# A gate for every gather in a graph network's edge loop

## The chip, the cores and the metric

The kernel runs on one core of a Trainium2 chip. The metric is the time of one execution on the device, in microseconds (us), as the median of several runs.

## The reference

One layer of a graph network on 6250 nodes with 256 features and 206250 edges, sorted by their destination. All numbers are 32-bit floats.

```
h    = relu(layernorm(x))
e    = relu(raw @ W_e1.T + b_e1) @ W_e2.T + b_e2          # raw: 64 features of an edge
edge = (e * (clip(polarity, 0, 1) + 0.01)) @ W_le.T + b_le
msg  = relu(h[src] + edge)                                # one row gathered for each edge
aggr = segment_sum(msg, dst)
g    = layernorm((h + aggr) @ W_g1.T + b_g1) * ln_g + ln_b
out  = x + relu(g) @ W_g2.T + b_g2
```

## The kernel before

**Staging.** A first stage normalizes the nodes and writes `relu(layernorm(x)) + b_le` to a table in HBM, `hb_d`. W_e2 and W_le are multiplied into one matrix `wc_s`. The edges are cut into 403 blocks of 512 edges (4 tiles of 128). A *unit* is half a block, 256 edges; there are NU = 806 units, and the edge loop goes once through them. Two blocks make a pair (4 units), 6 blocks make a group, whose sums come out together. `LEAD` = 22 units are computed ahead, during the first stage.

**The work of a unit.** `edge_part(u)` runs 8 matmul instructions on TensorE (L268) into a PSUM tile `pz`, which VectorE empties into `msg` (L273). Every pair needs a first layer on TensorE before (`first_layer`, L245), which fills four `pz` tiles; ScalarE (L253) and VectorE (L250) empty them. In the middle of the loop (`by_two`) first layers come for two pairs at once, every 8 units: this is called a *turn* here, and its run of L245 has 16 instructions and needs 8 tiles. There are 7 `pz` tiles. Behind the first layers of a turn stand the sums of two pairs (`add_pairs`, `add_up`, L583: 8 instructions a block) and the loads of two more pairs (`load_pair`, on SyncE's queue).

**The gathers.** Each unit needs two indirect DMAs of 128 rows from `hb_d` into a tile `hg` (L531), issued by GpSimd. `whole(u)` then adds the gathered rows to the messages on VectorE (L566, twice a unit, in place in `hg`) and applies relu on ScalarE (L571); the sums on TensorE (L583) read `hg`, and then its buffer is free. There are `HG` = 16 buffers of two gathers.

**The order of work.** The order on each engine is the order in which the program is written; no scheduler moves anything. An engine carries out its instructions in order, and waits where a semaphore has not come far enough. In the loop over u, `forward(u)` writes the unit's matmuls (and the turn's, when it is one), then `gathers(...)` writes the gathers that are now due, then `whole(made)` follows for a unit that lies behind u by a distance that shrinks from 22 to 1 in the course of the loop, and `due()` writes at most one step of the nodes' work (TensorE's L682, L166, L182, L192), which starts when the sums of a group are there.

**The gates.** `gathers(last, behind)` issues gathers up to unit `last`. The first gather of a call gets a made-up dependency on `behind`, here `last_z`, the last matmul of the unit: GpSimd may not start it sooner. In the middle of the loop the limit is

```
k = (u - TURN) % 8
gathers(4 * summed + HG - 8 + (1, 2, 3, 4, 5, 6, 6, 7)[k], last_z)
```

so that gathers are issued for buffers that the sums have freed, spread over the 8 units of a turn. Before the loop, `gathers(HG)` issues the first 32 gathers without a gate. In the last 24 units gathers have no gate either. Beside the gate a gather waits for its buffer, and for the landing of the gather 8 places before it.

Of the kernel before, what the change touches and what calls it, by code (L numbers as in the profile page):

```python
# [17 lines left out]
P = 128  # L18
N = 6250
D = 256  # L20
F = 64
# [7 lines left out]
S = 4  # L29
L = 6  # L30
W = 32
# [7 lines left out]
DEG = E // N  # L39
LEAD = 22  # L40
LEAST = 1
SHRINK = 36
HG = 16
FEW = 6
QUIET = (0, 1)
TURN = 1
# [5 lines left out]
def group_of(b):  # L52
    return b // L


def blocks_of(g):
    return range(g * L, min((g + 1) * L, NB))
# [36 lines left out]
def gnn_kernel(ctx: ExitStack, tc: tile.TileContext, x, src_c, dst_c, dst_r, pol_c, raw_t, w_e1t, w_e2,  # L94
               w_let, w_g1t, w_g2t, vec_c, row_v, x_t, out):
    nc = tc.nc
# [3 lines left out]
    hb_d = dram.tile([N, D], F32, name="hb_d")  # L100
# [14 lines left out]
    we1_s = const.tile([P, D], F32, name="we1_s")  # L115
    wc_s = const.tile([P, 2, D], F32, name="wc_s")
    bc_s = const.tile([P, 2, D], F32, name="bc_s")
    src_s = const.tile([P, NT], I32, name="src_s")
# [92 lines left out]
    NU = 2 * NB  # L211
    fast = ExitStack()
    fast.enter_context(tc.manual_schedule())
    with fast:
# [8 lines left out]
        raw, sel, e1, hg, msg, ms = {}, {}, {}, {}, {}, {}  # L223
        pd = psd.tile([P, 2, D], F32, name="pd")

        def ps():
            return psz.tile([P, 2, D], F32, name="pz")
# [6 lines left out]
        def first_layer(q):  # L234

            bs = [b for b in (2 * q, 2 * q + 1) if b < NB]
            if not bs:
                return
            for b in bs:
                e1[b] = e1_p.tile([P, 2, 512], F32, name="e1")  # L240
            pe = {}
            for c in range(2):
                for s, b in enumerate(bs):
                    pe[s, c] = ps().rearrange("p a b -> p (a b)")
                    nc.tensor.matmul(pe[s, c], we1_s[s * F:(s + 1) * F, c * P:(c + 1) * P],  # L245
                                     raw[q][s * F:(s + 1) * F, :], start=True, stop=True)
            for c in range(2):
                for s, b in enumerate(bs):
                    if s == c == 1:
                        nc.vector.tensor_scalar(e1[b][:, c, :], pe[s, c], be1_s[:, c:c + 1], 0.0, op0=ALU.add,  # L250
                                                op1=ALU.max)
                    else:
                        nc.scalar.activation(e1[b][:, c, :], pe[s, c], AF.Relu, bias=be1_s[:, c:c + 1])  # L253
            raw.pop(q)

        def plain(u):

            return u < LEAD and u % 3 == 1

        def edge_part(u):  # L260

            nonlocal last_z
            b, v = divmod(u, 2)
            pz = ps()
            for i in range(2):
                k = (2 * v + i) * P
                for c in range(2):
                    last_z = nc.tensor.matmul(pz[:, i, :], e1[b][:, c, k:k + P], wc_s[:, c, :], start=c == 0, stop=c == 1)  # L268
            msg[u] = msg_p.tile([P, 2, D], F32, name="msg")
            if plain(u):  # L270
                nc.scalar.activation(msg[u], pz, AF.Copy)
            else:
                nc.vector.tensor_add(msg[u], pz, bc_s)  # L273
            if v == 1:
                e1.pop(b)

        last_z = None
        sums = lambda last: None

        def by_two(q):  # L280
            return FEW <= q < NP - FEW
# [16 lines left out]
        def forward(u):  # L298

            edge_part(u)  # L300
            if u % 4 == TURN:
                turn_of(u // 4)
# [33 lines left out]
        with tc.tile_pool(name="p1", bufs=4) as p1, tc.tile_pool(name="p1x", bufs=11) as p1x:  # L336
# [76 lines left out]
            for k in range(len(parts) + 1):  # L413
# [15 lines left out]
                for _ in range((k > 0) + (k > 2 and k % 3 > 0)):  # L429
                    u = next(units, None)  # L430
# [85 lines left out]
        with tc.tile_pool(name="hg", bufs=HG) as hg_p, tc.tile_pool(name="ms", bufs=5) as ms_p, \  # L516
                tc.tile_pool(name="sel2", bufs=9) as sel2_p, tc.tile_pool(name="nd", bufs=3) as nd:
            got = 0
            acc = {}
            made = 0  # L520
            summed = 0

            def gathers(last, behind=None):

                nonlocal got
                while got < min(NU, last):
                    u = got
                    got += 1
                    hg[u] = hg_p.tile([P, 2, D], F32, name="hg")
                    for i in range(2):  # L530
                        g = nc.gpsimd.indirect_dma_start(  # L531
                            out=hg[u][:, i, :], out_offset=None, in_=hb_d,
                            in_offset=bass.IndirectOffsetOnAxis(ap=src_s[:, 2 * u + i:2 * u + i + 1], axis=0))
                        if behind is not None:
                            tc.add_manual_dep(g.ins, behind.ins.name, mybir.DependencyInfo(
                                mybir.DependencyClass.Sync, mybir.DependencyReason.DATA), reason="gathers in step with PE")
                            behind = None

            def select(g):

                return [(g, lambda k=k: rows_of_block(g, k)) for k in range(len(blocks_of(g)))]

            def rows_of_block(g, k):

                t = (g * L + k) * S
                if k == 0:
                    sel[g] = sel_p.tile([P, L * S, W], F32, name="sel")
                nc.vector.scalar_tensor_tensor(  # L548
                    sel[g][:, k * S:(k + 1) * S, :], iota_w.rearrange("p (o w) -> p o w", o=1).to_broadcast([P, S, W]),
                    zero_c, rel[:, t:t + S].rearrange("p (t o) -> p t o", o=1).to_broadcast([P, S, W]), op0=ALU.add,  # L550
                    op1=ALU.is_equal)
# [8 lines left out]
            def whole(u):  # L560

                m = msg.pop(u)
                if plain(u):
                    nc.vector.tensor_add(m, m, bc_s)
                for i in range(2):
                    nc.vector.scalar_tensor_tensor(hg[u][:, i, :], m[:, i, :], pol_s[:, 2 * u + i:2 * u + i + 1],  # L566
                                                   hg[u][:, i, :], op0=ALU.mult, op1=ALU.add)
                    if u == NU - 1:
                        nc.scalar.activation(hg[u][:, i, :], hg[u][:, i, :], AF.Relu)
                if u < NU - 1:  # L570
                    nc.scalar.activation(hg[u], hg[u], AF.Relu)  # L571

            def add_up(b):

                g = group_of(b)
                k = b - g * L
                if k == 0:
                    acc[g] = pd[:, g % 2, :] if g < NG - 1 else ps()[:, 0, :]
                    while rest and rest[0][0] <= g:
                        rest.popleft()[1]()  # L580
                for j in range(S):
                    m = hg[2 * b + j // 2]
                    nc.tensor.matmul(acc[g][j * W:(j + 1) * W, :], sel[g][:, k * S + j, :], m[:, j % 2, :],  # L583
                                     start=k == 0, stop=b == blocks_of(g)[-1])
                hg.pop(2 * b)
                hg.pop(2 * b + 1)
                return g if b == blocks_of(g)[-1] else None

            def keep(g):
# [37 lines left out]
            def at(u, fn):  # L627
                todo.setdefault(max(u, now), deque()).append(fn)
# [81 lines left out]

            def due():

                fns = todo.pop(now, deque())
                if fns and not (by_two(now // 4) and now % 8 in QUIET):
                    fns.popleft()()
                if fns:
                    todo.setdefault(now + 1, deque()).extendleft(reversed(fns))

            gathers(HG)
            sums = add_pairs  # L720
            for i, fn in ((0, first_rows), (1, rows_of_edges), (3, lambda: rest.extend(select(0) + select(1))), (5, row_numbers), (6, stats_out),
                          (8, node_weights)):
                at(LEAD + i, fn)
# [4 lines left out]
            for u in range(LEAD, NU):  # L728
                now = u
                forward(u)  # L730

                if u >= NU - 24:
                    gathers(4 * summed + HG)
                elif by_two(u // 4):
                    k = (u - TURN) % 8
                    gathers(4 * summed + HG - 8 + (1, 2, 3, 4, 5, 6, 6, 7)[k], last_z)
                else:
                    gathers(4 * summed + HG - 4 + (u - TURN) % 4 + 1, last_z)

                piece()  # L740
                while made < u + 1 - max(LEAST, LEAD - u // SHRINK) - (by_two(u // 4) and (u + 1) % 8 == TURN):
                    whole(made)
                    made += 1
                due()
                if len(rest) > 6:
                    piece()
                if u == NU - 24:
                    for w in range(NW):
                        if groups_of(w)[-1] == NG - 1:
                            late[w] = node_work(w, True)  # L750
                if u == LEAD + 60:
                    flag = nc.values_load(bad_i[0:1, 0:1], min_val=0, max_val=3 * P)
# [6 lines left out]
            before, last = ending[-2], ending[-1]  # L759
# [192 lines left out]
```

## Time and profile before

| what | before |
|---|---|
| median of 3 runs (lowest to highest) | 2172.71 us (2172.22 to 2173.83) |
| the profiled execution: its time | 2171.32 us |
| its span, first to last instruction | 2169.5 us |
| granted TensorE clock | 0.997 |
| VectorE busy, ScalarE busy | 77%, 44% |
| DMA engines busy, from 66 to 300 us | 46%, 138 GB/s |
| first and last gather start | 63.3 us, 2148.0 us |
| a gather on GpSimd (lowest, median, highest) | 0.942, 0.949, 2.235 us |

PE is TensorE, DVE VectorE, ACT ScalarE, POOL GpSimd, SP SyncE; L268 is line 268 of the kernel before. A group's row gives the line, the engine, the operation, the tiles written and read and the count; then the busy time, the mean duration of one in ns, and the engine's idle time ahead of it with what ended it. In a list of waits a row gives who waited for whom, the us in total, how often, and the longest. In a timeline a row gives the start, the duration, the engine and the instruction, and in brackets the idle time ahead of it. A matmul's recorded duration holds its way through the array, so that matmuls overlap in the records: L268 takes 0.381 us by the record, and one starts every 0.216 us. A gather's record on GpSimd ends when the transfer has been issued; it lands later, at the median 2.80 us after its start.

### The profile page before, as it was taken

How to read it: one execution, taken by the hardware profiler on the slowest of the kernel's cores; microseconds unless marked ns; L12 is line 12 of the kernel's file. 1: busy time of each engine (PE TensorE's matmuls, PEld its weight loads, DVE VectorE, ACT ScalarE, POOL GpSimd, SP SyncE). 2: the span in 40 equal slices, each digit the busy share in tenths (PEclk: the TensorE clock that was granted, in tenths of full speed). 3: DMA queues.
4: the chain of work that ended last, by engine and by line, in shares of the span. 5: the costliest groups of instructions: out<-in, count | busy, mean ns of one | idle time of the engine just before them, and what ended most of it. 6: DMA issues, size and time to landing. Idle time of an engine off the chain costs nothing.

```text
span 2169.5 us, 35373 instructions
## 1 busy us (share of the span) xinstructions
PE 2155.0 (99%) x12382; PEld 1616.9 (75%) x12382; DVE 1677.7 (77%) x3953; ACT 964.0 (44%) x1701; POOL 1619.4 (75%) x1675
## 2 busy tenths in 40 slices
PE   9999999999999999999999999999999999999998
PEld 7677777777777777777777777777777777777776
DVE  7788777878777777877777787777777777777786
ACT  7444444444444444444444444443434444443443
POOL 5777777777777777777777777777777777777774
PEclk9999999999999999999999999999999999999999
DMA  9544445444444454544454445444544544454442
GB/s 319 157 133 137 134 131 157 135 140 144 142 121 145 145 148 127 151 134 139 129 152 142 132 131 162 130 117 148 152 134 124 155 134 146 131 154 124 139 138 84
DMA packets 156079, 309.20 MB, mean 143 GB/s; under 512 B 33183, under 2 KB 77944, under 8 KB 155896
## 3 DMA queue, kind: packets, MB, share of 16 engines
q0 software_dynamic: 77376, 211.39, 33.5%
q1 hardware_dynamic: 77364, 92.23, 13.3%
q10 hardware_dynamic: 1156, 3.28, 0.4%
q8 instruction: 98, 1.61, 0.3%
q14 instruction: 85, 0.70, 0.1%
HBM read 293.92 MB, written 12.85 MB: 141 GB/s over the span
## 4 chain that ended last, share of the span: by engine, by line
PE 92%; DMA 1%; POOL 1%; DVE 1%; issue 1%; ACT 0%; SPq 0%; POOLq 0%; DVEq 0%; ACTq 0%
PE pz L268 60%; PE pz L245 16%; PE pd L583 9%; PE pz L682 3%; PE pz L192 2%; PE pz L166 2%; DMA hg<-hb_d,src_s 1%; POOL hg L531 1%; PE pz L182 1%; DVE hg L566 0%; DVE msg L273 0%; DMA hb_d<-hb 0%; ACT e L253 0%; DVE st L137 0%; PE pz L666 0%
## 5 line engine op out<-in xcount | busy, mean ns | idle before, releaser
L531 POOL DMA_INDIRECT hg<-hb_d,src_s x1612 | 1582.1, 981 | 505.7 <-issue 358.5
L268 PE MATMUL pz<-wc_s,e 128*128 128x256 f32 x6448 | 1451.8, 381 | 0.0
L268 PEld LDWEIGHTS pz<-wc_s,e 128*128 128x128 f32 x6448 | 1208.9, 190 | 202.0 <-issue 33.8
L571 ACT ACTIVATE hg<-hg 128x512 f32<-128x512 f32 x805 | 502.2, 629 | 988.5 <-DVE hg L566 980.7
L566 DVE SCALAR_TENSOR_TENSOR hg<-msg,pol_s,hg 128x256 f32<-128x256 f32 x1612 | 699.1, 478 | 38.6 <-DMA hg<-hb_d,src_s 37.7
L273 DVE TENSOR_TENSOR msg<-pz,bc_s 128x512 f32<-128x512 f32 x799 | 547.8, 686 | 226.6 <-PE pz L268 226.4
L253 ACT ACTIVATE e<-pz,vecs 128x512 f32<-128x512 f32 x605 | 361.3, 692 | 127.8 <-PE pz L245 127.7
L245 PE MATMUL pz<-raw,we_s 64*128 64x512 f32 x1612 | 389.7, 607 | 4.4 <-DVE msg L273 4.0
L245 PEld LDWEIGHTS pz<-raw,we_s 64*128 64x128 f32 x1612 | 152.4, 187 | 187.9 <-issue 137.3
L250 DVE TENSOR_SCALAR e<-pz,vecs 128x512 f32<-128x512 f32 x201 | 150.6, 749 | 183.0 <-PE pz L245 183.0
L583 PE MATMUL pd<-hg,sel 128*32 128x256 f32 x3216 | 195.7, 384 | 0.0
L583 PEld LDWEIGHTS pd<-hg,sel 128*32 128x32 f32 x3216 | 94.7, 110 | 128.4 <-issue 77.1
L548 DVE SCALAR_TENSOR_TENSOR sel<-iota_w,zero_c,rel 128x128 f32<-128x128 f32 x403 | 137.8, 342 | 2.3 <-PE pd L583 2.3
L682 PEld LDWEIGHTS pz<-s,ms 128*128 128x128 f32 x548 | 68.7, 192 | 3.1 <-PE pd L583 0.4
L682 PE MATMUL pz<-s,ms 128*128 128x128 f32 x548 | 69.3, 275 | 0.1
L657 DVE SCALAR_TENSOR_TENSOR hT<-hT,zero_c,stb 128x128 f32<-128x128 f32 (+1 forms) x196 | 67.0, 342 | 0.9 <-DMA stb<-st_d 0.9
L373 POOL TENSOR_TENSOR hb<-xt,rows_b 128x256 f32<-128x256 f32 (+1 forms) x49 | 34.2, 729 | 23.1 <-ACT xt L369 14.8
L192 PE MATMUL pz<-wg_s,nT 128*128 128x256 f32 (+1 forms) x196 | 50.5, 380 | 0.5 <-ACT nT L185 0.5
L166 PE MATMUL pz<-wg_s,hT 128*128 128x256 f32 (+1 forms) x196 | 50.5, 380 | 0.0
L594 ACT ACTIVATE ms<-pd 128x256 f32<-128x256 f32 x66 | 25.4, 384 | 51.7 <-PE pd L583 51.7
L192 PEld LDWEIGHTS pz<-wg_s,nT 128*128 128x128 f32 (+1 forms) x196 | 37.0, 190 | 6.2 <-ACT nT L185 0.7
L166 PEld LDWEIGHTS pz<-wg_s,hT 128*128 128x128 f32 (+1 forms) x196 | 37.0, 190 | 5.7 <-issue 0.3
(91 smaller groups left out, 393.1 us busy)
## 6 DMA issues: line engine op xcount, KB each, us to landing
raw<-in_raw_t_dram SPq DMA_DIRECT2D x202, 256.0 KB
hg<-hb_d,src_s POOLq DMA_INDIRECT x1612
stb<-st_d SPq DMA_DIRECT2D x49, 128.0 KB
hb_d<-hb SPq DMA_DIRECT2D x12, 512.0 KB
xt<-in_x_dram SPq DMA_DIRECT2D x48, 128.0 KB
hT<-in_x_t_dram SPq DMA_DIRECT2D x48, 128.0 KB
out_dram<-ot SPq DMA_DIRECT2D x48, 128.0 KB
xt<-in_x_dram SPq DMA_DIRECT2D x11, 512.0 KB
```

What stands on the lines that cost most here:

```text
L166: nc.tensor.matmul(ph[:n, 0, :], aT[:, c, :n], wg1_s[:, c, :], start=c == 0 and not bias_by_pe, stop=c == 1)
L245: nc.tensor.matmul(pe[s, c], we1_s[s * F:(s + 1) * F, c * P:(c + 1) * P], raw[q][s * F:(s + 1) * F, :], start=True, stop=True)
L250: nc.vector.tensor_scalar(e1[b][:, c, :], pe[s, c], be1_s[:, c:c + 1], 0.0, op0=ALU.add, op1=ALU.max)
L253: nc.scalar.activation(e1[b][:, c, :], pe[s, c], AF.Relu, bias=be1_s[:, c:c + 1])
L268: last_z = nc.tensor.matmul(pz[:, i, :], e1[b][:, c, k:k + P], wc_s[:, c, :], start=c == 0, stop=c == 1)
L273: nc.vector.tensor_add(msg[u], pz, bc_s)
L531: g = nc.gpsimd.indirect_dma_start(out=hg[u][:, i, :], out_offset=None, in_=hb_d, in_offset=bass.IndirectOffsetOnAxis(ap=src_s[:, 2 * u + ...
L548: nc.vector.scalar_tensor_tensor(sel[g][:, k * S:(k + 1) * S, :], iota_w.rearrange("p (o w) -> p o w", o=1).to_broadcast([P, S, W]), zero_ ...
L566: nc.vector.scalar_tensor_tensor(hg[u][:, i, :], m[:, i, :], pol_s[:, 2 * u + i:2 * u + i + 1], hg[u][:, i, :], op0=ALU.mult, op1=ALU.add)
L571: nc.scalar.activation(hg[u], hg[u], AF.Relu)
L583: nc.tensor.matmul(acc[g][j * W:(j + 1) * W, :], sel[g][:, k * S + j, :], m[:, j % 2, :], start=k == 0, stop=b == blocks_of(g)[-1])
L682: nc.tensor.matmul(pa[:, c, :n], ms[g][:, c * P:(c + 1) * P], box["sel2"][i][:, :n], start=i == 0, stop=i == len(gs) - 1)
```

## The change

A running account `spent` adds up TensorE's work by an estimate: 1.754 us for a unit (`EDGE`), 0.9 for each half of a pair's first layer (`LAYER`), 0.46 for the sums of a block (`SUMS`), 0.65 for a step of the nodes' work (`NODES`). After each of the first three, `in_step` issues gathers, singly and no longer by units, until the number issued times `STEP` = 1.285 us has reached `spent` + `AFLOAT` (2.6 us). The first gather that such a call issues waits for the matmul at which the account stands. The buffers limit them as before (`4 * summed + HG` units). Only one unit's gathers go out ahead of the loop. The limits of the loop before go; where `whole(made)` is written and its gathers are not yet, `gathers(made + 1)` issues them without a gate. The last 24 units stay without gates.

```diff
+EDGE, LAYER, SUMS, NODES = 1.754, 0.9, 0.46, 0.65
+STEP = 1.285
+AFLOAT = 2.6
...
@@ def first_layer(q):
-                    nc.tensor.matmul(pe[s, c], we1_s[s * F:(s + 1) * F, c * P:(c + 1) * P],
-                                     raw[q][s * F:(s + 1) * F, :], start=True, stop=True)
+                    z = nc.tensor.matmul(pe[s, c], we1_s[s * F:(s + 1) * F, c * P:(c + 1) * P],
+                                         raw[q][s * F:(s + 1) * F, :], start=True, stop=True)
+                paced(LAYER, z)
...
@@ def edge_part(u):
+            paced(EDGE, last_z)
...
-            def gathers(last, behind=None):
+            def gather(behind=None):
                 nonlocal got
-                while got < min(NU, last):
-                    u = got
-                    got += 1
+                u, i = divmod(got, 2)
+                got += 1
+                if i == 0:
                     hg[u] = hg_p.tile([P, 2, D], F32, name="hg")
...
+            def gathers(last):
+                while got < 2 * min(NU, last):
+                    gather()
+
+            def in_step(us, behind):
+                nonlocal spent
+                spent += us
+                while got * STEP < spent + AFLOAT and got < 2 * min(NU, 4 * summed + HG):
+                    gather(behind)
+                    behind = None
...
@@ def add_up(b):
+                paced(SUMS, z)
...
@@ def due():
+                    spent += NODES
...
-            gathers(HG)
+            gathers(1)
             sums = add_pairs
+            paced = in_step
...
                 if u >= NU - 24:
                     gathers(4 * summed + HG)
-                elif by_two(u // 4):
-                    k = (u - TURN) % 8
-                    gathers(4 * summed + HG - 8 + (1, 2, 3, 4, 5, 6, 6, 7)[k], last_z)
-                else:
-                    gathers(4 * summed + HG - 4 + (u - TURN) % 4 + 1, last_z)
 
                 piece()
                 while made < u + 1 - max(LEAST, LEAD - u // SHRINK) - (by_two(u // 4) and (u + 1) % 8 == TURN):
+                    gathers(made + 1)
                     whole(made)
```

More of the change, by code (lines that the diff above doesn't have):

```diff
@@ L275, in edge_part @@
                 e1.pop(b)
+            paced(EDGE, last_z)
         last_z = None
         sums = lambda last: None
+        paced = lambda us, behind: None
         def by_two(q):
@@ L521, in gnn_kernel @@
             summed = 0
-            def gathers(last, behind=None):
+            spent = 0.0
+            def gather(behind=None):
                 nonlocal got
-                while got < min(NU, last):
-                    u = got
-                    got += 1
+                u, i = divmod(got, 2)
+                got += 1
+                if i == 0:
                     hg[u] = hg_p.tile([P, 2, D], F32, name="hg")
[L530 to L537, printed above, removed]
+                g = nc.gpsimd.indirect_dma_start(
+                    out=hg[u][:, i, :], out_offset=None, in_=hb_d,
+                    in_offset=bass.IndirectOffsetOnAxis(ap=src_s[:, 2 * u + i:2 * u + i + 1], axis=0))
+                if behind is not None:
+                    tc.add_manual_dep(g.ins, behind.ins.name, mybir.DependencyInfo(
+                        mybir.DependencyClass.Sync, mybir.DependencyReason.DATA), reason="gathers in step with PE")
+            def gathers(last):
[7 more added lines that the diff above has]
+                    behind = None
             def select(g):
@@ L582, in add_up @@
                     m = hg[2 * b + j // 2]
-                    nc.tensor.matmul(acc[g][j * W:(j + 1) * W, :], sel[g][:, k * S + j, :], m[:, j % 2, :],
-                                     start=k == 0, stop=b == blocks_of(g)[-1])
+                    z = nc.tensor.matmul(acc[g][j * W:(j + 1) * W, :], sel[g][:, k * S + j, :], m[:, j % 2, :],
+                                         start=k == 0, stop=b == blocks_of(g)[-1])
                 hg.pop(2 * b)
                 hg.pop(2 * b + 1)
+                paced(SUMS, z)
                 return g if b == blocks_of(g)[-1] else None
@@ L711, in due @@
             def due():
+                nonlocal spent
                 fns = todo.pop(now, deque())
                 if fns and not (by_two(now // 4) and now % 8 in QUIET):
+                    spent += NODES
                     fns.popleft()()
```

## The prediction

> **What bounds the kernel now.** I read the page's busy times and chain first, then the costliest groups, the waits of VectorE and GpSimd, and the timeline where a wait reaches TensorE.
>
> ```profile
> PE 2155.0 (99%) x12382; PEld 1616.9 (75%) x12382; DVE 1677.7 (77%) x3953; ACT 964.0 (44%) x1701; POOL 1619.4 (75%) x1675
> ...
> PE 92%; DMA 1%; POOL 1%; DVE 1%; issue 1%; ACT 0%; SPq 0%; POOLq 0%; DVEq 0%; ACTq 0%
> ...
> L531 POOL DMA_INDIRECT hg<-hb_d,src_s x1612 | 1582.1, 981 | 505.7 <-issue 358.5
> ```
>
> TensorE holds 92% of the chain that ended last. But GpSimd, at 75%, is nearly as full: 1612 gathers take 0.981 us each, and the records show 0.305 us between two of them, whatever comes next. That is 1.286 us a gather, 2073 us in all, and the gathers run from 63.3 to 2148.0. By the records, the gaps hold only 12.7 us beyond the usual 0.305, nearly all of it in 19 places. So two engines keep the same pace, and the gathers are a queue that is almost never empty.
>
> ```profile
> DVE hg L566 <- DMA hg<-hb_d,src_s: 37.7, 42, 2.6
> ```
>
> This row of VectorE's waits says that 42 uses of gathered rows came too early, by 37.7 us together. How that reaches TensorE shows in the timeline of one turn (columns: start us, us, engine, line):
>
> ```profile
> 1003.51 0.47 DVE L566 SCALAR_TENSOR_TENSOR hg<-msg,pol_s,hg 128x256 f32<-128x256 f32 x1
> ...
> 1005.94 0.48 DVE L566 SCALAR_TENSOR_TENSOR hg<-msg,pol_s,hg 128x256 f32<-128x256 f32 x1 [1.96 <-DMA hg<-hb_d,src_s]
> ...
> 1006.34 0.68 DVE L273 TENSOR_TENSOR msg<-pz,bc_s 128x512 f32<-128x512 f32 x1
> ```
>
> VectorE works in order, so while it waits 1.96 us for a gather, the L273 behind it doesn't empty its PSUM tile. The next first-layer run (L245) needs the tiles:
>
> ```profile
> 986.89 3.70 PE L245 MATMUL pz<-raw,we_s 64*128 64x512 f32 x16
> ...
> 1007.27 4.40 PE L245 MATMUL pz<-raw,we_s 64*128 64x512 f32 x16
> ```
>
> An undisturbed run of 16 takes 3.70 us, this one 4.40. Summed over all runs from 60 us on, L245 loses 18.6 us in this way.
>
> **The change, part by part.** On TensorE, VectorE, ScalarE and SyncE the order of instructions and their waits stay what they were. GpSimd issues the same 1612 gathers in the same order; its load of the flag (L752) moves ahead of two of them, and no gap over 0.4 us stands there now, so I cost that at nothing: the flag is computed some units earlier, and if that cover were missing it would cost GpSimd the same wait, not another. No DMA is added. What changes is what gathers wait for: by the semaphores that the two programs name, 787 of them wait for TensorE before and 1181 after. Taking for each gather the last matmul that it or one ahead of it waits for, the new gate is a later matmul for 1553 gathers, the same for 59, an earlier one for none. **So with unchanged durations every instruction starts at the same time or later**; a gain can only come from shorter gathers or landings.
>
> *Satisfied waits.* The gap before a gather is 0.305 us with a satisfied TensorE wait and 0.305 without: nothing, covered by that gap.
>
> *Binding waits.* Where a wait held a gather in this trace, it started 0.74 us (9 times) or 0.95 (7 times) after the recorded end of its matmul. I take 0.74. Behind a waiting gather GpSimd has only more gathers; VectorE's L566 waits for them, L273 behind that, L245 behind that.
>
> *The estimate itself.* It is fair: EDGE 1.754 against 8 matmuls at 0.216 (1.73); four LAYER 3.6 against 3.70; four SUMS 1.84 against 1.93 for 32 L583; NODES 0.65 against some 160 us of L682, L166, L182 and L192 over 245 calls; STEP 1.285 against 1.286. So gates come at the very pace at which GpSimd works. An unhindered gather takes 0.949 + 0.305 = 1.254 us: a queue that has lost 1 us needs 1 / (1.286 - 1.254) = 31 gathers, two turns of the loop, to win it back.
>
> *Where the gates fall.* The old gates ended at the median 5.1 us ahead of the start of their gather (5% to 95%: 10.2 to 1.2 us ahead): a reserve of some four gathers. The new gates, put on the recorded TensorE times, lie at the median 0.12 us **behind** the recorded start of the same gather (5% to 95%: 1.83 ahead to 1.83 behind). Carrying the queue forward over the recorded times (each gather at the later of its gate plus 0.74 and its predecessor plus 0.305, with its recorded duration), gathers start 1.12 to 3.64 us later than recorded, median 2.63. The time from landing to use falls from a median 3.69 us to 1.21, and 446 of 1612 uses come too early, where there were 42.
>
> *The beginning.* Today 32 gathers go out ungated from 63.3 us. Then gather 3 waits for a unit that ends at 66.45: 66.45 + 0.74 - 65.97 = 1.2 us late. Gather 30 waits for 104.53: 104.53 + 0.74 - 102.96 = 2.3 us late, and by gather 35 it is 3.0. GpSimd had no gap from there to 295.2, so up to 3 us stay; between nothing (landing to use is 1.6 us at the lower quartile there) and 3.0 + 1.2 = 4.2 us. It is contained in the next sum.
>
> *The turns.* There are 99 stretches between first-layer runs. For each I took the latest landing against its use, over all chains that begin at a gate at most 42 us earlier (two turns): gate + 0.74 + the gathers from there + landing. VectorE makes up part of that. From turns where it waited: 2.62 us of waiting lengthened L245 by 0.78, 2.82 by 0.69, 2.73 by 0.70, 4.32 by 2.24: cover 1.8 to 2.1; others (1.72 by 1.49, 2.03 by 1.56) show 0.2 to 0.5. I take 1.5, nearer to the larger group. What is over 1.5 us sums to 20.7 us with the recorded landings and to 6.3 with all landings at their median (1.82 us after the gather's end); the truth lies between, since a TensorE that is held also gives some of today's 18.6 us back. The middle is **13.5 us**. With cover 1.0 and recorded landings it is 42.2, with cover 2.0 and median landings 1.7.
>
> Sum: profiled time 2171.3 + 13.5 = 2184.8, bounds 2173.0 and 2213.5. The median of the runs is 1.4 us over the profiled time: **2186**, 2174 to 2215.
>
> **The rivals.**
> *The cover holds (0.14).* VectorE is 77% busy and catches up ahead of each L245, so only what GpSimd itself stands idle is lost: in the carried queue it waits 15.2 us at gates, against 12.7 us of excess gaps now. That is 2.5 us, 2175, between 2174 (1.7 us) and 2177. For it: 1.286 of the 1.294 us between two starts are GpSimd's own, and the turn that ended at 243 us had 1.3 us of waiting and lost nothing. Against: TensorE's work is as tight, and a TensorE that is held moves the gates too.
> [...]
>
> *Faster (0.09): gathers get shorter.* 333 gathers take over 1.0 us, together 51.5 us more than 0.949 each for all; L566 runs over 61% of their time, and over 28% of that of the short ones. If gates move gathers out of L566's way, the queue runs ahead of need and L245 gets back up to 18.6 us; half of it gives 2163. It decides where the mean gather falls under 0.97 us. Against: both instructions are as many as before and nearly back to back, so what leaves one L566 meets the next.
> [...]
>
> *Worse (0.07).* Late gathers fall more often into SyncE's loads: 224 gathers landed over 3 us after their end, against 1.82. Cover 1.0 and more such landings: over 2215.
>
> *The gates don't act* is part of the first: then GpSimd's excess gap stays near 12.7 us.
>
> **How the numbers follow.** Forecast 0.70, of which 0.04 stays under 0.2% (4.3 us, about what a measurement of this kernel tells from no change). Slower: 0.66 + 0.07 = 0.73. Same: 0.14 + 0.04 = 0.18. Faster: 0.09. The range runs from 2170, which takes in part of the third case, to 2215; it leaves out 0.07 above and 0.06 below.
>
> **What would show it.** Right: GpSimd's waits on PE well over today's, VectorE's wait for gathers above 37.7 us in more than 42 places, L245 runs longer than 3.70 in more turns, the mean gather still at 0.98, L268 still 0.216 us a matmul. Wrong: fewer waits at L566, or a shorter gather; or waits at L566 that L245 doesn't feel, which is the first rival.

## The result, and the profile after

| | before | after |
|---|---|---|
| median (lowest to highest; 4 runs each) | 2172.47 us (2170.64 to 2173.83) | 2204.71 us (2200.24 to 2205.92) |
| profiled execution, its span | 2171.32, 2169.5 us | 2203.99, 2202.2 us |
| granted TensorE clock | 0.997 | 0.995 |
| first and last gather start | 63.3, 2148.0 us | 64.5, 2183.8 us |

The change makes the kernel slower: the ratio is 1.0145, 95% interval 1.0128 to 1.0163. The forecast was 13.5 us over before; 32.2 were measured, inside the range of 2170 to 2215. The lines moved: L245 of before is L248 after, L268 is L272, L273 L277, L531 L537, L566 L584, L583 L601. The page of after, in the rows that were shown of before:

```profile
PE 2180.1 (99%) x12382; PEld 1623.1 (74%) x12382; DVE 1682.0 (76%) x3953; ACT 961.9 (44%) x1701; POOL 1612.3 (73%) x1675
...
PE 87%; DMA 3%; DVE 2%; issue 1%; POOL 1%; ACT 0%; POOLq 0%; DVEq 0%; ACTq 0%
...
L537 POOL DMA_INDIRECT hg<-hb_d,src_s x1612 | 1575.0, 977 | 548.0 <-issue 356.8
```

TensorE's busy share reads 99% in both and so doesn't show the loss; a matmul's record lasts longer than the distance of two starts (L272: 0.381 us for 0.216; L248: 0.589 for 0.227), and a hold shorter than the difference leaves no idle time in the records. The chain tells more: TensorE's part falls from 92% to 87%, while that of the gathers' landings (DMA) rises from 1% to 3% and VectorE's from 1% to 2%. A gather is no longer than it was (0.977 for 0.981 us), but GpSimd is idle 548.0 us ahead of them where it was 505.7. VectorE's waits, in the row that was shown of before (37.7 us in 42 places):

```profile
DVE hg L584 <- DMA hg<-hb_d,src_s: 144.0, 185, 3.0
```

and what TensorE itself waited for (before: 4.0 us, 7 times):

```profile
PE pz L248 <- DVE msg L277: 10.3, 20, 1.5
```

One turn shows how this becomes time (timeline of after; start us, us, engine, line):

```profile
2058.95 0.49 DVE L584 SCALAR_TENSOR_TENSOR hg<-msg,pol_s,hg 128x256 f32<-128x256 f32 x1 [2.27 <-DMA hg<-hb_d,src_s]
...
2060.82 1.99 PE L248 MATMUL pz<-raw,we_s 64*128 64x512 f32 x8
2061.57 0.95 DVE L584 SCALAR_TENSOR_TENSOR hg<-msg,pol_s,hg 128x256 f32<-128x256 f32 x2 [1.27 <-DMA hg<-hb_d,src_s]
...
2063.17 1.12 PE L248 MATMUL pz<-raw,we_s 64*128 64x512 f32 x2 [0.36 <-DVE msg L277]
...
2064.82 2.45 PE L248 MATMUL pz<-raw,we_s 64*128 64x512 f32 x6 [0.53 <-DVE msg L277]
...
2067.20 3.11 PE L601 MATMUL pd<-hg,sel 128*32 128x256 f32 x32
```

VectorE waits 2.27 and 1.27 us for rows. The L277 behind those waits empty PSUM tiles late, and the first-layer run, undisturbed one piece of 3.70 us, breaks into 8, 2 and 6 instructions and lasts from 2060.82 to 2067.27. The sums behind it take 3.11 us where 32 take 1.93, for a reason that the table by stretches shows (columns: the engines' busy us, then PEclk, the granted clock, the DMA share and GB/s):

```profile
2056.00:2061.00 5.00, 5.00 (x25) 4.15 (x25) 2.02 (x6) 0.63 (x1) 3.78 (x5) 1.00 0.88 294
2061.00:2066.00 5.00, 4.11 (x14) 1.40 (x15) 4.43 (x10) 2.37 (x5) 3.78 (x5) 1.00 0.59 187
2066.00:2069.40 3.40, 3.40 (x28) 1.06 (x28) 2.35 (x6) 2.36 (x5) 2.46 (x3) 0.53 0.59 156
```

From 2066.22 on, still within the disturbed run, TensorE gets half the clock for 3.4 us. The first row also shows what goes with the late rows just here: the DMA engines were 88% busy, at 294 GB/s. SyncE had issued eight loads from 2052 to 2057 us (`raw`, and node rows), and the five gathers that ended on GpSimd between 2054.0 and 2059.1 landed 4.1 to 6.2 us later, where the median is 1.83. This holds over the whole loop: from 110 us on, 74 gathers landed over 4 us after their end, and in the 3 us behind their end the DMA engines were 87% busy on average, against 34% behind gathers that landed within 2.2 us. But the change didn't make these landings late. Gathers of the same turn landed up to 6.0 us after their end before, too; they had started earlier against their use.

Summed over the trace, the first-layer runs from 60 us on lose 47.8 us over their undisturbed time, where they lost 18.6. That is 29.2 of the 32.7 us by which the span grew, and the sums (L601) lose 3.5 us more than before, which is the rest.

### The profile page after: what moved, and what is told of

Same layout as the page of the kernel before. It is cut to its first block, busy times and chain, and to the rows that moved or that the text cites. A ratio compares the mean times of both kernels' runs of the same rounds, so it can differ in the third digit from the quotient of the medians.

```text
span 2202.2 us, 35947 instructions
## 1 busy us (share of the span) xinstructions
PE 2180.1 (99%) x12382; PEld 1623.1 (74%) x12382; DVE 1682.0 (76%) x3953; ACT 961.9 (44%) x1701; POOL 1612.3 (73%) x1675
## 4 chain that ended last, share of the span: by engine, by line
PE 87%; DMA 3%; DVE 2%; issue 1%; POOL 1%; ACT 0%; POOLq 0%; DVEq 0%; ACTq 0%
PE pz L272 57%; PE pz L248 15%; PE pd L601 8%; PE pz L701 3%; DMA hg<-hb_d,src_s 3%; PE pz L169 2%; PE pz L195 2%; DVE msg L277 1%; POOL hg L537 1%; DVE hg L584 1%; PE pz L185 0%; DVE hT L676 0%; DVE st L140 0%; PE pz L685 0%; PE pz L167 0%
## 5 line engine op out<-in xcount | busy, mean ns | idle before, releaser
L537 POOL DMA_INDIRECT hg<-hb_d,src_s x1612 | 1575.0, 977 | 548.0 <-issue 356.8
L272 PE MATMUL pz<-wc_s,e 128*128 128x256 f32 x6448 | 1451.8, 381 | 1.5 <-ACT msg L275 1.5
L272 PEld LDWEIGHTS pz<-wc_s,e 128*128 128x128 f32 x6448 | 1208.8, 190 | 203.9 <-issue 28.6
L584 DVE SCALAR_TENSOR_TENSOR hg<-msg,pol_s,hg 128x256 f32<-128x256 f32 x1612 | 712.7, 481 | 147.6 <-DMA hg<-hb_d,src_s 144.0
L277 DVE TENSOR_TENSOR msg<-pz,bc_s 128x512 f32<-128x512 f32 x799 | 547.8, 687 | 184.8 <-PE pz L272 184.3
L248 PE MATMUL pz<-raw,we_s 64*128 64x512 f32 x1612 | 411.5, 611 | 11.2 <-DVE msg L277 10.3
L248 PEld LDWEIGHTS pz<-raw,we_s 64*128 64x128 f32 x1612 | 157.8, 186 | 209.5 <-issue 111.7
L601 PE MATMUL pd<-hg,sel 128*32 128x256 f32 x3216 | 199.3, 389 | 0.0
L601 PEld LDWEIGHTS pd<-hg,sel 128*32 128x32 f32 x3216 | 95.7, 111 | 132.0 <-issue 82.0
L566 DVE SCALAR_TENSOR_TENSOR sel<-iota_w,zero_c,rel 128x128 f32<-128x128 f32 x403 | 138.7, 344 | 2.4 <-PE pd L601 2.3
```

Source lines behind the costliest of these rows:

```text
L248: z = nc.tensor.matmul(pe[s, c], we1_s[s * F:(s + 1) * F, c * P:(c + 1) * P], raw[q][s * F:(s + 1) * F, :], start=True, stop=True)
L537: g = nc.gpsimd.indirect_dma_start(out=hg[u][:, i, :], out_offset=None, in_=hb_d, in_offset=bass.IndirectOffsetOnAxis(ap=src_s[:, 2 * u + ...
L566: nc.vector.scalar_tensor_tensor(sel[g][:, k * S:(k + 1) * S, :], iota_w.rearrange("p (o w) -> p o w", o=1).to_broadcast([P, S, W]), zero_ ...
L601: z = nc.tensor.matmul(acc[g][j * W:(j + 1) * W, :], sel[g][:, k * S + j, :], m[:, j % 2, :], start=k == 0, stop=b == blocks_of(g)[-1])
```

## The experiments

Theory A: the loss is lost lead. Gathers that follow TensorE at 2.6 us leave their rows too little time before their use. Theory B: the loss is in the number of gates, each with its own wake. Later two finer ones were set against each other: G, GpSimd is so full that it never makes up what a gate held it, and L, the lead is too short at each turn by itself. Theory C is about two chips on which time goes another way; they come last. Most texts on record give times for a chip where before takes 2171 to 2172 us. Each run stands beside runs of the kernel before on its own chip; "over before" is the difference of these medians.

| kernel | lead | gates | median | ratio to before (95%) | over before | VectorE's waits for gathers | loss of first-layer runs |
|---|---|---|---|---|---|---|---|
| before | some 5 us | 787 | 2172.47 | 1 | 0 | 37.7 us, 42 | 18.6 us |
| changed | 2.6 | 1181 | 2204.71 | 1.0145 (1.0128 to 1.0163) | 32.2 | 144.0, 185 | 47.8 |
| float_4 | 3.9 | 1164 | 2176.59 | 1.0022 (1.0012 to 1.0032) | 4.2 | 69.6, 85 | 24.8 |
| float_5 | 5.2 | 1127 | 2172.59 | 1.0009 (0.9999 to 1.0018) | 2.0 | 42.4, 57 | 19.2 |
| float_10_third | 10.3 | 895 | 2172.11 | 1.0009 (0.9999 to 1.0018) | 1.5 | 44.4, 55 | 20.3 |
| early_10 | 10.3, then 2.6 | 1146 | 2189.01 | 1.0081 (1.0064 to 1.0098) | 18.4 | 124.7, 169 | 34.9 |
| pair_gates | 2.6 | 801 | 2203.39 | 1.0135 (1.0108 to 1.0162) | 31.0 | 142.1, 189 | 48.2 |
| pairs_later | before's, less 2.57 | 682 | 2260.57 | 1.0406 (1.0380 to 1.0432) | 90.0 | 188.2, 248 | 96.3 |
| thin_after | 2.6 | 1142 | 2190.36 | 1.0086 (1.0067 to 1.0104) | 18.0 | 95.7, 137 | 34.7 |
| thin_before | before's | 787 | 2167.89 | 0.9978 (0.9969 to 0.9988) | -4.5 | 22.0, 26 | 15.6 |

"Gates" is the number of gathers with a TensorE wait by the program; the last two columns are of the profiled execution, the losses summed as for before and after. The leads are not all on one scale: that of a changed kernel is its `AFLOAT`, in us of the account, and that of before is the median distance from a gate to the start of its gather, by which the changed kernel's gates were put at 0.12 us behind. What rows had left in the end, from landing to use, is at the median 3.69 us before, 1.66 in the changed kernel, 2.58 in float_4, 3.18 in float_5 and in float_10_third, 1.63 in pair_gates and 2.01 in pairs_later.

**More lead, the gates kept: float_5, float_10_third, float_4.**

```diff
-AFLOAT = 2.6
+AFLOAT = 5.2        # float_5; 10.3 in float_10_third, 3.9 in float_4
```

> AFLOAT 5.2 for 2.6: every gate two distances of 1.285 us earlier, 1,127 gates for 1,181. Theory A (the loss of the change is lost lead: rows land too close to their use): most of the 32 us come back, 2178 to 2190 us on a chip where before takes 2172, ratio 1.003 to 1.008. Theory B (the loss is the number of waiting gathers, some 0.4 us of wake at each binding wait): nearly all of it stays, ratio 1.012 to 1.015. On a chip where before takes some 2580 us (TensorE's results late there): theory C (the more densely and early the gathers run, the later the results) wants it between the changed kernel and the one with 10.3, near 1.00 to 1.03.

> AFLOAT 10.3 again, for a chip on which TensorE's results are not late. There theory A: about before, 2168 to 2178 us, ratio 0.998 to 1.003; theory B (895 gates for 787): 1.003 to 1.008. On a chip where before takes some 2580 us: 1.06 as in the two measurements.

> AFLOAT 3.9, one distance more than in the changed kernel, one less than in the run that equalled before. Theory A: between them and nearer to the good end, since what is late at a turn falls faster than the lead rises (by the lateness of the recorded landings, 29 us at a cover of 1.25 and 20.7 at 1.5): 2175 to 2188 us, ratio 1.002 to 1.008. If there is a threshold at the wake and the landing (0.74 + 0.98 + 1.83 = 3.55 us from the gate to the rows), it is all back: 2169 to 2175.

With 5.2 us the loss is gone (2.0 us, and the interval touches 1; less stayed than the text had wanted, 2178 to 2190), with nearly all of the single gates still there. So A holds, and B falls: a gate as such costs nothing that shows. Only 27 gathers were held here, by over 0.1 us beyond the usual gap, where the changed kernel had 85: at 5.2 us of lead hardly a gate holds. The row of VectorE's waits is nearly that of before:

```profile
DVE hg L584 <- DMA hg<-hb_d,src_s: 42.4, 57, 2.6
```

A lead of 10.3 us gives nothing more (the rows had the same 3.18 us left), and 3.9 us already brings back 28 of the 32 us, so the loss is steep: 1.3 us of lead are worth 28 us, the next 1.3 some 2. Between the wake, the gather and its landing lie 0.74 + 0.98 + 1.83 = 3.55 us. That a lead over that sum is nearly enough fits these points, but they don't prove a threshold: the text wanted 2169 to 2175 us for one, and 2176.59 came. And a lead in us of the account isn't the time from a gate to the use of its rows.

**More lead at the beginning alone: early_10.**

```diff
-                while got * STEP < spent + AFLOAT and got < 2 * min(NU, 4 * summed + HG):
+                while got * STEP < spent + (10.3 if now < 110 else AFLOAT) and got < 2 * min(NU, 4 * summed + HG):
```

> A lead of 10.3 us for the units up to 110, 2.6 after them: undoes the change's lateness in the first 300 us alone. Theory A, with the 16.8 us that the stretches of the first 400 us lost: 2188 to 2194 us where before takes 2172, ratio 1.007 to 1.010. Theory B: 2200 to 2204, ratio 1.013 to 1.015. On a chip where before takes some 2580 us, theory C: a little slower than the changed kernel (0.983 of before), 0.985 to 1.00, since only some 80 gathers run ahead.

18.4 us over before instead of 32.2: some 14 us of the loss belong to the beginning. The changed kernel's trace agrees: matmul by matmul, its L272 is 1.3 us behind L268 of before at 100 us, 14.4 at 300 and 17.5 at 400. The other 16 of its 33 us build up over the 1750 us that follow.

**The same lead with half of the gates: pair_gates.**

```diff
                     gather(behind)
+                    gather()
                     behind = None
```

> The changed kernel, but only the first gather of a unit has a gate, at its own due time, and the second follows it: 801 gates for 1,181. On GpSimd a gather and its gap last 1.286 us, the distance of the gates 1.285, so the second starts where its gate would have let it. Theory A (lost lead): 2196 to 2206 us where before takes 2171, ratio 1.012 to 1.016. Theory B (each gate of its own costs, by its wake or by work that TensorE does less evenly than the estimate): 2184 to 2194, 1.006 to 1.011.

The second gather of each unit has no gate, and nothing changes: 31.0 us over before, the intervals of the two ratios overlap, and VectorE's row is the changed kernel's:

```profile
DVE hg L585 <- DMA hg<-hb_d,src_s: 142.1, 189, 3.1
```

Whether each gather has its own gate doesn't matter; where the gates lie does. Nearly as many gathers were held as in the changed kernel (72 for 85), so this run says nothing on the price of a hold.

**The old gates with less lead: pairs_later.** The kernel before, its limits lowered by one unit (and `gathers(made + 1)` ahead of `whole(made)`, as in the changed kernel):

```diff
-                    gathers(4 * summed + HG - 8 + (1, 2, 3, 4, 5, 6, 6, 7)[k], last_z)
+                    gathers(4 * summed + HG - 10 + (1, 2, 3, 4, 5, 6, 6, 7)[k], last_z)
...
-                    gathers(4 * summed + HG - 4 + (u - TURN) % 4 + 1, last_z)
+                    gathers(4 * summed + HG - 6 + (u - TURN) % 4 + 1, last_z)
```

> The kernel before with its own gates, in pairs, and its limit lowered by one unit (two gathers, 2.57 us), so its lead is about the changed kernel's; fewer waits than before (682 for 787). Theory A: the loss comes without the change's single gates, 2190 to 2206 us where before takes 2172, ratio 1.008 to 1.015. Theory B: 2168 to 2176, ratio 0.998 to 1.002. On a chip where before takes some 2580 us, theory C: faster than before, 0.975 to 0.995, since its gathers run later, as the changed kernel's do; if evenness is what gains there, 0.998 to 1.005.

The sign is A's, but the size was missed: 90 us, not 18 to 35. The old gates hang on the units alone. While TensorE does the first layers and sums of a turn, no gate is reached, and without the lead GpSimd runs dry (timeline of pairs_later; the number in brackets is the idle time ahead):

```profile
702.81 0.95 POOL L531 DMA_INDIRECT hg<-hb_d,src_s  x1 [0.30 <-issue]
705.44 2.33 PE L583 MATMUL pd<-hg,sel 128*32 128x256 f32 x32
...
707.70 3.72 PE L268 MATMUL pz<-wc_s,e 128*128 128x256 f32 x16
...
710.44 1.06 POOL L531 DMA_INDIRECT hg<-hb_d,src_s  x1 [6.68 <-issue]
```

GpSimd starts again when the first unit behind the turn is done: 707.70, plus 8 matmuls at 0.216 us, 0.16 by which the last one's record (0.381) is longer than that, and 0.74 for the wake, is 710.3. There are 32 gaps of over 1.5 us beyond the usual 0.305 here, 91.3 us together; in the changed kernel there are 3, of 5.2 us. So at a short lead the change's even gates are the better ones (32 us lost against 90, though the rows of pairs_later had more time left at the median, 2.01 us against 1.66), and at a long lead they bring nothing.

**More time for GpSimd: thin_after, thin_before.** In both kernels one gather in sixteen becomes a plain load from ScalarE's queue; those messages are not the reference's. A gate that stood at such a gather goes to the next in thin_after:

```diff
+                if u >= 32 and 2 * u % 16 == 0 and i == 1:
+                    nc.scalar.dma_start(out=hg[u][:, i, :], in_=hb_d[:P, :])
+                    return behind
                 g = nc.gpsimd.indirect_dma_start(
```

> The changed kernel with 97 of the 1,612 gathers (one in sixteen, from unit 32 on) replaced by a plain load of 128 fixed rows from the Activation queue: the messages of those edges are not the reference's. GpSimd needs 97 x 1.286 = 125 us less, all gates stay (a gate that would have stood at a replaced gather goes to the next). Theory G (GpSimd is as full as TensorE, 2073 us of work in some 2085, so that what a gate holds it is never made up): with the slack the loss goes, 2165 to 2180 us, within 8 us of thin_before. Theory L (the lead of 2.6 us is too short at each turn by itself, however much time GpSimd has): 20 us and more of the 32 stay, 2190 to 2205.

> The kernel before with the same 97 gathers replaced. Both theories: 2160 to 2172 us where before takes 2171, since its gathers hold TensorE little; the difference to thin_after is what counts. If one more load on the Activation queue costs something, both of the pair show it.

With 125 us less for GpSimd to do, the changed kernel is still 2190.36 - 2167.89 = 22.5 us behind. So by this pair L has the larger part, some 22 of 32 us, and G some 10. (A load in place of 97 gathers may itself shorten landings, and ScalarE waits 14.8 us behind landings of these loads in thin_after, 4.7 in thin_before; the pair doesn't separate either.) VectorE still waits in the thinned kernel with the short lead, and hardly in the other:

```profile
DVE hg L586 <- DMA hg<-hb_d,src_s: 95.7, 137, 2.5
```

```profile
DVE hg L569 <- DMA hg<-hb_d,src_s: 22.0, 26, 2.3
```

thin_before is 4.5 us faster than before. That many us, no more, this edit gets from giving GpSimd time; with the lead that before has, its gathers cost little.

**On two other chips.** The eight runs before these fell on two chips where the kernel before takes 2609 and 2579 us, at granted clocks of 0.95 to 0.96. Each chip was met once, so that the chip and the moment aren't told apart. There the order is another, and the times in the first four texts, meant for a chip like the first, were all missed:

| kernel | lead | ratio to before there (95%) | median there |
|---|---|---|---|
| changed_again | 2.6 | 0.9834 (0.9797 to 0.9872) | 2530.29 (before 2579.28) |
| before_again | before's | profile only | 2569.44 |
| early_float | 40, from unit 150 on 2.6 | 1.0294 (1.0261 to 1.0326) | 2686.84 (before 2609.29) |
| float_10 | 10.3 | 1.0593 (1.0567 to 1.0620) | 2763.31 (before 2609.29) |
| float_10_again | 10.3 | 1.0633 (1.0602 to 1.0665) | 2738.99 (before 2579.28) |
| late_float | 2.6, from unit 150 on 40 | 1.2070 (1.2038 to 1.2101) | 3149.39 (before 2609.29) |
| float_buffers | up to the buffers | 1.2569 (1.2513 to 1.2625) | 3270.14 (before 2609.29) |
| float_buffers_again | up to the buffers | 1.2561 (1.2512 to 1.2610) | 3237.09 (before 2579.28) |

The edits are of the one term: `AFLOAT = 10.3`; `AFLOAT = 1e6` (float_buffers, 207 gates); `spent + (40.0 if now < 150 else AFLOAT)` (early_float); `spent + (AFLOAT if now < 150 else 40.0)` (late_float). The kernels named "again" repeat the edit named.

> The changed kernel with AFLOAT at a million: the account never holds a gather, only the 16 buffers do, and 207 gathers wait for TensorE in place of 1181. Theory (the gates took away the lead that the gathers had on their use): the lead from landing to use comes back to a median of 3.7 us or more from 1.7, VectorE's waits for gathers fall from 144 us to 40 or less, and the time to 2172, give or take 5. Rival (pacing itself is worth something, and gathers in bursts behind the sums land among the loads): landings over 3 us after the gather's end rise well over 240, time between 2180 and 2200.

> AFLOAT 10.3 in place of 2.6: the same single gates, each 7.7 us of the account (6 gathers) earlier; 895 gathers still wait for TensorE. Theory (lost lead): nearly all comes back, 2172 to 2178, GpSimd's gaps beyond 0.305 us fall from 54.6 us to some 15. Rival (each wait costs GpSimd time, whatever its lead): 895 of 1181 waits are left, so some three quarters of the 32 us stay, 2192 to 2200.

> Gates held open (float 40) for the units up to 149, as in the changed kernel from there on. In the traces 16.8 of the 32 us are lost before 400 us, which is where these units end. If each stretch loses on its own, this saves about 16 us: 2188. If a lead lost at any time is paid once and a lead kept early carries through, more: 2180. If the steady turns alone count, as the predicted sum had it with 4 us at most for the beginning: 2200.

> The opposite half: the changed kernel's gates up to unit 149, then a float of 40. If each stretch loses on its own: 2204 - 16 = 2188, and together with the run that opens the first half the two savings add up to the whole 32 us. If the early loss is only a delay that a later lead gives back: 2175 to 2180.

> The changed kernel itself, beside the kernel before on one chip. The first four experiments met a chip on which the kernel before takes 2609 us, TensorE's results come late by the semaphores, and every kernel with an earlier gather was the slower one. If that belongs to the chip, then where the kernel before takes 2172 this one takes 2204 again (ratio 1.0145); and on a chip like the last one this kernel, whose gathers start latest, is the faster: ratio 0.94 to 1.00. If the pacing is what both chips answer to, the ratio is the same on both.

> The kernel before itself, for its trace on the same chip. Where it takes 2172: VectorE starts within 0.3 us of the TensorE results that it waits for, as in the first trace. On a chip like the last one: results that are late by several us here too, so that the gathers' order is not what makes them late.

> AFLOAT 10.3 in place of 2.6, the same single gates 7.7 us of the account earlier. On a chip where the kernel before takes 2172: theory (lost lead) 2172 to 2178, GpSimd's gaps beyond 0.305 us back to some 15 us; rival (each of the 895 waits left costs GpSimd time): 2192 to 2200. On a chip like the last one: about 1.06 times the kernel before again.

> AFLOAT a million, so that the buffers alone hold gathers. On a chip where the kernel before takes 2172: theory (lost lead) 2172, give or take 5; rival (pacing is worth something by itself) 2180 to 2200. On a chip like the last one: about 1.26 times the kernel before again.

On its chip float_10_third equals before; here the same kernel is 6% slower, and the more lead, the slower. Gathers that come late are not the reason. In before_again VectorE hardly waits for them:

```profile
DVE hg L566 <- DMA hg<-hb_d,src_s: 9.1, 10, 2.1
```

TensorE itself is slow (timeline of before_again, TensorE alone):

```profile
363.93 0.46 PE L268 MATMUL pz<-wc_s,e 128*128 128x256 f32 x1
364.63 0.38 PE L268 MATMUL pz<-wc_s,e 128*128 128x256 f32 x1 [0.24 <-issue]
365.35 0.91 PE L268 MATMUL pz<-wc_s,e 128*128 128x256 f32 x3 [0.34 <-issue]
366.76 1.02 PE L268 MATMUL pz<-wc_s,e 128*128 128x256 f32 x4 [0.50 <-issue]
368.20 1.12 PE L268 MATMUL pz<-wc_s,e 128*128 128x256 f32 x4 [0.41 <-issue]
369.62 0.81 PE L268 MATMUL pz<-wc_s,e 128*128 128x256 f32 x3 [0.30 <-issue]
```

and its clock in that stretch (the same columns as above):

```profile
365.00:375.00 10.00, 6.32 (x24) 4.09 (x23) 0.00 (x0) 0.00 (x0) 7.56 (x9) 1.00 0.36 105
```

TensorE starts 24 records in 10 us where 46 at 0.216 us would fit. They come in groups of about four, 1.4 us apart, with no wait that the profile shows, and the granted clock is recorded as 1.00. What the others see is that TensorE's results come late. Counting the stretches of over 3.8 us between two of its semaphore updates (a unit needs 1.73 us), 892 us lie in them in before_again, 791 in changed_again, 1055 in float_10_again, 1570 in float_buffers_again, and 5 us in before and in after on the chip of the first measurement. The times follow that order. So does the half clock, which by the records lasts 197, 159, 417 and 979 us in these four: it is a second part of the loss. Theory C, that gathers which run densely and early set it off, has this order for it; in float_buffers_again gathers start at 0.69 a us inside those stretches against 0.50 overall, but in before_again it is 0.64 against 0.63. So C isn't shown. What holds TensorE back on these chips stays open, and it can't explain the first result, which has none of it.

## Why the prediction was right or wrong

**What bounds the kernel: right.** TensorE, through first-layer runs that VectorE holds up. 29.2 of 32.7 us of the span came in these runs, and L272 still starts a matmul every 0.216 us.

**Later gates, unchanged durations, hence not faster: right.** The mean gather is 0.977 us (0.981 before), landings come at the median 1.83 us after a gather's end (1.82). The rival in which gathers shrink decided at 0.97 and did not come about. GpSimd's gaps beyond 0.305 us rose from 12.7 us in 19 places to 54.6 in 85, so the gates act.

**Binding waits: right.** 43 of the 85 held gathers started 0.74 us after their matmul's recorded end.

**The fall of the lead: right in kind, a little too dark.** Landing to use was to fall from a median of 3.69 us to 1.21; it fell to 1.66. 446 uses were to come too early; VectorE waited at 185. The difference is TensorE's own: where it was late, so was the use.

**The beginning: mis-sized.** It had at most 4.2 us, and by early_10 it is worth some 14. The step bounded one queue's delay, not what each turn makes of it: up to 400 us, eight first-layer runs lose 1.4 to 3.4 us each behind the first one at 91 us, which loses over 5 in both kernels. That VectorE has work of its own there that comes at the beginning alone, such as two reductions of 1.83 us (L494 of before, at 155.5 and 170.1), may add to it; no run separates this.

**The turns: the step that failed.** The sum with recorded landings was 20.7 us, and the forecast lowered it to 13.5, towards 6.3, "since a TensorE that is held also gives some of today's 18.6 us back". Next to nothing was given back: run by run, 1.4 of the 18.6 us went (1.2 of them in one run), 30.6 were added, and 18.6 became 47.8. Taking all landings at their median was the wrong bound, because late landings come in clusters (4.1 to 6.2 us, five in a row, in the turn shown), and a cluster is what goes over the cover.

Beyond 20.7 the sum lacked the half clock after a stall: three stretches of 3.4 us that before doesn't have, each 1.7 us lost by estimate (half of 3.4), 5.1 together; the 3.5 us that the sums L601 lose more than before hold most of it. With these the sum would have been 25.8 of the measured 32.2. The other 6 us lie in the first-layer runs too, since these and the sums make up the whole 32.7. Why the late rows cost more there than the sum had stays open.

The cover of 1.5 us isn't confirmed. In the trace after, what VectorE waited for gathers in each turn beyond 1.5 us sums to 46 to 49 us, by where a turn is taken to begin, near the 47.8 lost; but in the trace before it sums to 8 to 12, where 18.6 were lost. So not all of the 18.6 us were waits for gathers that went over a cover, as the prediction read them: the run at 157 us lost 1.56 us behind two waits of 0.46 and 0.65 and the reduction of 1.83 us on VectorE (L494).

**The cover holds (rival): wrong.** GpSimd's idle time alone was to be lost, 2.5 us. The last gather starts 35.8 us later, which is 1.2 at the start plus 41.9 of added gaps less 7 us of shorter gathers; but those gaps are, as far as the 29.2 us in TensorE's first-layer runs tell, mostly TensorE's lateness come back through the gates. What spoke for it, a GpSimd that is full (1.286 of the 1.294 us between two starts), does not carry the loss either: with 97 gathers fewer, 125 us at 1.286 each, thin_after is still 22.5 us behind thin_before.

## What to carry to other kernels

Price a gate by the time from it to the use of the rows, against the chain behind it (here wake, gather and landing, 3.55 us at their medians), and take the landing times as they come in clusters beside other loads, not at their median. Here even gates were worth having only where the lead was short (32 us lost against 90); gates that came early enough cost nothing clear of noise, 1127 of them (1.0009, 0.9999 to 1.0018). A short forecast step that says "and some of it comes back" needs a row that shows it coming back.

## What the runs showed of the hardware

Some stalls of the first-layer runs came with a half clock, and the sums behind the one shown took 3.11 us for 1.93: after, three stretches of 3.4 us at a granted clock of 0.50 begin in or just behind disturbed runs (at 145, 216 and 2066 us), beside one of 6.8 us at 97 that before has too, and pairs_later has 13 stretches of half clock, 65.9 us in all, where float_10_third has 2, of 12.4. In the turn shown TensorE's longest recorded idle time ahead of the half clock is 0.53 us. Most disturbed runs are followed by none, not even the one at 1372 us, which lost 3.7 us; what sets the half clock off is not shown.

The changed kernel ranks differently on two chips: it is 1.45% slower than before on the first, and 1.66% faster on one where, in the stretch shown, TensorE starts its matmuls in groups 1.4 us apart.
